# Layer 0 of a convolution sequence: softmax denominators from a column of ones, block transposes on VectorE, and queries among the hidden units

## The chip, the cores and the metric

The kernel runs on one core of a Trainium2 chip. The metric is the device time of one execution in microseconds (us), the median of several runs. One further execution is recorded by the hardware profiler; durations of single instructions come from it.

The engines are TensorE (PE; its weight loads are shown as PEld), VectorE (DVE), ScalarE (ACT), GpSimd (POOL) and SyncE (SP, which here only starts transfers). They run side by side, each in the order of its own program, and wait for each other by semaphores.

## The reference

The input is `x` of 4 x 16 x 512 x 512 float32 (batch, channels, rows, columns). Four layers follow each other; the change touches layer 0 alone, a window attention block with a perceptron:

```python
x = x + depthwise3x3(x) + pos_b                       # position
y = affine(x)                                         # per token, 16 channels
win = 8 x 8 windows of y                              # 64 tokens each
q, k, v = heads(win @ qkv_w.T + qkv_b)                # 2 heads of 8 channels
attn = softmax((q * 8**-0.5) @ k.T)                   # 64 x 64 per window and head
x = x + (attn @ v) @ proj_w.T + proj_b
x = x + gelu(affine(x) @ fc1_w.T + fc1_b) @ fc2_w.T + fc2_b    # 64 hidden units
```

Layer 1 is a quantized 3x3 convolution with batch norm, layer 2 two 3x3 convolutions, layer 3 a convolution with a perceptron. They stand after layer 0 in `conv_layers`.

## The kernel before

`window_attention` computes layer 0 in 64 steps (`STEPS`). A step n takes, of all 4 images, 8 strips of rows and 16 channels, 8 rows by 64 columns: that is 8 windows per strip and image. In the tiles `u` counts the images and `vv` the pairs of strips, four each; `quad(i)` is a group of 32 partitions, two strips (`w`) of 16 channels. `NJ` is 8 windows, `T` 64 tokens, `N` 512.

[...] In the code before, `bank(0)` to `bank(3)` are the halves of two tiles of two banks, `pairs[0]` and `pairs[1]`; `bank(4)` to `bank(7)` are four tiles of one bank, `singles`.

The order of PE, DVE, ACT and SP is the order in which the code is written (`tc.manual_schedule`); the framework adds the semaphore waits. Step n works as follows.

- `values(k)` (k is 0 to 7: `vv = k // 2`, half of the windows) transposes four windows of `y2` on PE (L342) into bank 4 or 6; DVE copies the result to `yt` (L347).
- `scores(k)` multiplies keys by queries (L355), 16 matmuls into banks 0 to 3. ACT takes the exponential of each pair, 1024 elements (L363), to `e`.
- `attend(k)` multiplies `yt` by `e` (L374) into bank 4 or 6, and a matrix of ones, `own`, by `e` (L379) into bank 5 or 7: the denominators, repeated for every channel.
- `divide(k)` takes on ACT a logarithm (L388) and an exponential of its negative (L389), which is the reciprocal, and multiplies on DVE (L390) into `o`.
- `output(*last)` is the second half of the perceptron of step n-1: matmuls by `fc2` (L422), the sum on DVE (L427) into `xo`, and for odd n-1 the stores (`store`, `_store_block`, L92). Each stored block takes two transfers, one for even rows and one for odd.
- `turn_keys` (L314) brings the tokens of the next step into `y2` by transfers within the core.
- `queries(y, h)` computes, for head h, the next step's queries (L324) into banks 0 to 3; DVE empties banks 0 and 2 (L334), ACT banks 1 and 3 (L332), into `g`. It stands once before and once after the last `attend`.
- `project` multiplies `o` by the projection (L398) into banks 4 to 7; DVE adds to `y` (L403).
- Then 16 units of `hidden` (L411), each four matmuls into one of banks 4 to 7 and a gelu on ACT (L416), are strewn among 36 units of `depthwise` (L291), which compute the position term of step n+2 into banks 0 to 3.
- `position` empties banks 0 and 2 on DVE (L306) and 1 and 3 on ACT (L302) into `y`.

Two table loads per step on ACT switch between the exponential and the gelu. On DVE there are two more reductions, of the largest value of `y` (L504, `most`) and of the stored output (L442, `peak`), which later layers need.

## Time and profile before

| | us |
|---|---|
| median of 3 runs | 6021.88 |
| lowest and highest of them | 6014.76, 6022.8 |
| the profiled execution, its own time | 6030.1 |
| the span in its profile | 6028.3 |
| PE busy | 5775.3 (96%) |
| ACT busy | 3837.6 (64%) |
| DVE busy | 3268.4 (54%) |
| POOL busy | 171.1 (3%) |

A line of the timeline gives the start and length in us, the engine, the line of the code, the operation, what it writes and reads with the shapes, and how many instructions of that kind are merged; in brackets, the idle time ahead of it and what ended it. A line of the list of waits gives who waited for whom: us in total, how often, and the longest. A float32 matmul appears as two instructions (two passes). The clock granted to TensorE was 0.993 of full speed on the mean.

### The profile page before, as it was taken

Reading aid. Unit: us, or ns where it says so; the run is one execution under the profiler, and the core shown is the slowest. Engines: PE = TensorE matmul, PEld = TensorE weight load, DVE = VectorE, ACT = ScalarE, POOL = GpSimd, SP = SyncE. Lnnn points to the kernel's source line nnn. Section 1 sums busy time; section 2 is a strip of 40 time slices with the busy share of each in tenths; the row PEclk is TensorE's granted clock in tenths of the full one; section 3 lists DMA queues with packets and bytes.
Section 4 is the critical chain, followed back from the end, with each engine's and each line's share of the span. In section 5 each row is a group of like instructions: output and inputs, shape, how many; then the busy total and the mean of one; then the engine's idle time right before and its main releaser. Section 6 shows DMA issues by size and latency. Waiting matters only on the chain. (4 is left out here: it accounts for less than half of the span.)

```text
span 6028.3 us, 242228 instructions
## 1 busy us (share of the span) xinstructions
PE 5775.3 (96%) x108624; PEld 3084.9 (51%) x108624; DVE 3268.4 (54%) x4648; ACT 3837.6 (64%) x5257; POOL 171.1 (3%) x193
## 2 busy tenths in 40 slices
PE   8999999999999999999999866899999999999999
PEld 5666666666666666666666433333333333333333
DVE  3444444444444444444444455566666666666666
ACT  4777877877787777778777654344444444444444
POOL 0000000000000000000000154000000000000000
PEclk9999999999999999999999999999999999999999
DMA  3233333323333232333333398666676666666663
GB/s 84 58 71 66 64 77 62 78 59 71 67 64 77 61 79 59 71 66 65 77 61 61 58 243 216 163 171 168 167 173 165 168 172 166 168 171 168 167 170 104
DMA packets 638119, 674.57 MB, mean 112 GB/s; under 512 B 371728, under 2 KB 500880, under 8 KB 632976
## 3 DMA queue, kind: packets, MB, share of 16 engines
q1 hardware_dynamic: 635760, 657.53, 47.1%
q8 instruction: 857, 14.04, 1.0%
q0 software_dynamic: 1024, 1.05, 0.1%
q14 instruction: 190, 1.56, 0.1%
q10 hardware_dynamic: 288, 0.39, 0.0%
HBM read 221.15 MB, written 134.48 MB: 59 GB/s over the span
## 5 line engine op out<-in xcount | busy, mean ns | idle before, releaser
L363 ACT ACTIVATE e<-pair 128x1024 f32<-128x1024 f32 x1024 | 992.5, 1021 | 381.7 <-PE pair L355 381.7
L1175 ACT ACTIVATE hid<-tb,vec 128x512 f32<-128x512 f32 x1024 | 620.7, 688 | 517.5 <-PE tb L1167 517.4
L291 PE MATMUL pair<-x,taps 32*32 32x512 f32 x18432 | 927.4, 605 | 2.6 <-ACT y L302 1.2
L1177 DVE TENSOR_SCALAR hid<-tb,vec 128x512 f32<-128x512 f32 x1024 | 695.7, 742 | 2.7 <-PE tb L1167 2.6
L411 PE MATMUL bank<-y,fc_e 32*32 32x512 f32 x8192 | 680.1, 598 | 0.9 <-DVE y L403 0.9
L355 PE MATMUL pair<-g,y 32*128 32x128 f32 x16384 | 653.0, 285 | 26.9 <-ACT y L302 25.0
L355 PEld LDWEIGHTS pair<-g,y 32*128 32x128 f32 x16384 | 542.8, 186 | 215.9 <-issue 108.9
L416 ACT ACTIVATE hid<-bank,f1b 128x512 f32<-128x512 f32 x1024 | 644.5, 686 | 12.4 <-PE bank L411 4.8
L291 PEld LDWEIGHTS pair<-x,taps 32*32 32x32 f32 x18432 | 602.2, 103 | 98.2 <-issue 19.0
L347 DVE COPY yt<-bank 128x512 f32<-128x512 f32 x512 | 347.3, 688 | 540.2 <-PE bank L342 531.9
L1167 PE MATMUL tb<-ye,mat 32*128 32x512 f32 x4096 | 637.6, 624 | 0.3 <-DVE hid L1177 0.3
L374 PE MATMUL bank<-e,yt 128*32 128x128 f32 x16384 | 556.7, 276 | 3.4 <-issue 2.4
L390 DVE TENSOR_TENSOR o<-bank,r 128x512 f32<-128x512 f32 x512 | 354.2, 692 | 372.6 <-ACT r L389 356.3
L379 PE MATMUL bank<-e,hot 128*32 128x512 f32 x4096 | 535.6, 593 | 0.0
L1187 PE MATMUL tb<-hid,mat 128*32 128x512 f32 x4096 | 466.0, 595 | 41.6 <-DVE hid L1177 41.6
L374 PEld LDWEIGHTS bank<-e,yt 128*32 128x32 f32 x16384 | 418.0, 109 | 111.7 <-DVE yt L347 52.8
L306 DVE TENSOR_SCALAR y<-pair,vec 128x512 f32<-128x512 f32 x128 | 90.3, 746 | 706.5 <-PE pair L291 706.5
L1167 PEld LDWEIGHTS tb<-ye,mat 32*128 32x128 f32 x4096 | 267.0, 183 | 323.3 <-issue 219.9
L342 PEld LDWEIGHTS bank<-mat,y 128*128 128x128 f32 x2048 | 216.3, 141 | 376.1 <-issue 270.0
L1092 PE MATMUL tb<-zo,cw 64*32 64x512 f32 x3096 | 362.8, 594 | 14.9 <-issue 8.9
L1092 PE MATMUL tb<-xo,cw 64*32 64x512 f32 x3096 | 366.1, 600 | 10.1 <-issue 7.0
L1092 PE MATMUL tb<-xe,cw 64*32 64x512 f32 x3072 | 361.5, 600 | 0.0
(176 smaller groups left out, 7564.1 us busy)
## 6 DMA issues: line engine op xcount, KB each, us to landing
x<-in_xw_dram SPq DMA_DIRECT2D x32, 2600.0 KB, 10.9
zo<-ze SPq DMA_DIRECT2D x512, 128.5 KB, 2.4
ho<-he SPq DMA_DIRECT2D x512, 128.5 KB, 2.4
xo<-xe SPq DMA_DIRECT2D x512, 128.5 KB, 2.4
y<-y SPq DMA_DIRECT2D x2048, 32.0 KB, 2.2
tx<-x SPq DMA_DIRECT2D x256, 256.0 KB, 4.6
out_dram<-xe SPq DMA_DIRECT2D x128, 512.0 KB, 3.5
x<-xo SPq DMA_DIRECT2D x2016, 32.0 KB, 1.7
```

Source lines behind the costliest of these rows:

```text
L291: nc.tensor.matmul(bank(u)[quad(vv)], taps[quad(u), tap, :], xts[n // 2][quad(u), vv, dy : dy + WS, at : at + BW], start=tap == 0, stop=ta ...
L355: nc.tensor.matmul(bank(u)[:, P * jj : P * jj + P], y2[quad(u), vv, jl + jj].rearrange("p w t -> p (w t)"), g[quad(u), vv, jl + jj].rearra ...
L363: nc.scalar.activation(e[:, 2 * i : 2 * i + 2].rearrange("p u j t -> p u (j t)"), pairs[i], AF.Exp,)
L374: nc.tensor.matmul(b[quad(u), P * jj : P * jj + P], yt[:, jj, quad(u)], e[:, u, jj, :], start=True, stop=True,)
L379: nc.tensor.matmul(d[quad(u)], own, e[:, u].rearrange("p j t -> p (j t)"), start=True, stop=True,)
L411: nc.tensor.matmul(b[quad(k)], fc1[quad(vv), quad(k)], y[quad(vv), u, :], start=True, stop=True,)
L416: nc.scalar.activation(hd, b, AF.Gelu, bias=f1b)
L1092: nc.tensor.matmul(p[r][_quad(2 * f + w)], weights[_half(r), odd, dx, :], src[_half(r), f, dx : dx + W], start=dx == 0, stop=dx == 2,)
L1167: nc.tensor.matmul(p[q], w1[_quad(q), 1 - par, :], inner(src)[_quad(q), f, :], start=True, stop=True,)
L1175: nc.scalar.activation(hd, p[q], AF.Relu, bias=v("l3_b1"))
L1177: nc.vector.tensor_scalar(hd, p[q], v("l3_b1"), 0.0, ALU.add, ALU.max)
L1187: nc.tensor.matmul(p[r][_quad(c)], w2[:, par], hd, start=(r, c) not in seen, stop=(r, c) in seen,)
```

## The change

1. **Denominators.** `yts` are three fixed buffers of three column blocks for each quad: values of strip 0, ones, values of strip 1. A matmul by a neighbouring pair of these blocks gives sums and denominators together. `attend` now takes half the tokens (64 partitions, one strip) per matmul, 32 matmuls instead of 16 and no `own`; the strips go to the two banks of a pair.
2. **Division.** DVE transposes the whole pair in blocks of 32 x 32 (1024 elements per partition), so that tokens lie in the partitions, takes the reciprocal of the 32 denominators, GpSimd multiplies (DVE for k = 7), and `turn_back` transposes 512 elements back into `o`, one turn later. ACT's logarithm and exponential go. Four of eight copies of `values` move to ACT.
3. **PSUM.** Banks 4 to 7 become `pairs[2]` and `pairs[3]`.
4. **Queries.** `query` computes one head and one `vv`, with one DVE instruction to empty it. Eight of them stand among the hidden units; units take the banks 4, 5, 6, 7 in turn.
5. **Depthwise.** 16 of the 36 units move ahead of and behind the last `attend`.
6. **Reductions.** `most` moves behind `project`, `peak` to k = 2, 4, 6 and behind `most`.
7. **Transfers.** Inputs are loaded per step (half the width), stored blocks take one transfer each, spread by `send` over the turns.

```diff
-    n = WS // 2
-    m = r0 // 2
-    for r, mm in ((1, m), (0, m + 1)):
-        (next(queues) if queues else nc.sync).dma_start(
...
+    rows = x1.rearrange("m (r c) b x -> (m r) c b x", r=2)[r0 + 1 : r0 + 1 + WS, :, b, cols]
+    (next(queues) if queues else nc.sync).dma_start(rows.rearrange("m c x -> c m x"), src)
...
-    pairs = [ps.tile([P, 2, 512], F32, name=f"pair{i}") for i in range(2)]
-    singles = [ps.tile([P, 512], F32, name=f"bank{i}") for i in range(4)]
+    pairs = [ps.tile([P, 2, 512], F32, name=f"pair{i}") for i in range(4)]
     def bank(i):
-        return pairs[i // 2][:, i % 2, :] if i < 4 else singles[i - 4]
+        return pairs[i // 2][:, i % 2, :]
...
+    yts = [pa.tile([P, 4 * U, 3, C], F32, name=f"yt{i}") for i in range(3)]
+    for t in yts:
+        nc.gpsimd.memset(t, 1.0)
...
+    def query(y, h, vv, b):
         for u in range(U):
+            nc.tensor.matmul(
+                b[quad(u)], wg[h][quad(vv)], y[quad(vv), u, :], start=True, stop=True
+            )
+        nc.vector.tensor_scalar(
+            g[:, vv, :, h, :], b.rearrange("p (j t) -> p j t", t=T),
+            gb[:, h : h + 1], None, ALU.add,
+        )
...
+        src = b.rearrange("p (a w c) -> p a w c", w=2, c=C)
+        if k in (2, 4, 5, 6):
+            nc.scalar.copy(t[:, :, 0:3:2], src)
+        else:
+            nc.vector.tensor_copy(t[:, :, 0:3:2], src)
...
+    def attend(e, k):
+        t = yts[k % 3]
         for jj in range(4):
             for u in range(U):
+                for w in range(2):
+                    half = slice(64 * w, 64 * w + 64)
+                    nc.tensor.matmul(
+                        bank(4 + 2 * (k % 2) + w)[quad(u), P * jj : P * jj + P],
+                        t[half, U * jj + u, w : w + 2].rearrange("p d c -> p (d c)"),
+                        e[half, u, jj, :],
+                        start=True, stop=True,
+                    )
...
+    def divide(k, n, engine):
+        a = px.tile([P, 1024 + 2 * C], F32, tag="a", name=f"a{n}_{k}")
+        nc.vector.transpose(a[:, 0:1024], pairs[2 + k % 2].rearrange("p w n -> p (w n)"))
...
+        nc.vector.reciprocal(r, low)
+        t = px.tile([P, 16, 2, C], F32, tag="t", name=f"t{n}_{k}")
+        engine.tensor_tensor(
+            t.rearrange("p b w c -> p w b c"), top,
+            r.unsqueeze(3).to_broadcast([P, 2, 16, C]), ALU.mult,
+        )
+        return t
+
+    def turn_back(t, k):
+        nc.vector.transpose(part(o, k), t.rearrange("p b w c -> p (b w c)"))
...
         for k in range(1, 8):
             es[k] = scores(k, n)
             if k > 1:
+                values(k)
+            attend(es[k - 1], k - 1)
+            ts[k - 1] = divide(k - 1, n, nc.gpsimd)
+            if k > 1:
+                turn_back(ts[k - 2], k - 2)
+            if k % 2 and more:
                 turn_keys(ys[n + 1], k // 2)
+            if k in (2, 4, 6):
+                highest_output()
+            send(5)
+        turn_back(ts[6], 6)
+        rounds(1)
+        attend(es[7], 7)
+        turn_back(divide(7, n, nc.vector), 7)
+        rounds(3)
         y = ys.pop(n)
         project(y)
+        if more:
+            highest(n + 1)
+        highest_output()
...
+        hids, asked, units = [], 0, itertools.cycle(range(4, 8))
+        for what in "dddd" + 4 * "hdhqdhdhqd":
+            if what == "h":
                 q = len(hids)
+                hids.append(hidden(y, q, bank(next(units)), n))
...
+            elif what == "q" and more:
+                query(ys[n + 1], asked // V, asked % V, bank(next(units)))
+                asked += 1
+            elif what == "d" and ahead:
+                u = taken.index(min(taken))
+                depthwise(n + 2, taken[u], u)
+                taken[u] += 1
```

More of the change, by code (lines that the diff above doesn't have):

```diff
@@ L87, in _store_block @@
 def _store_block(nc, x1, src, b, r0, cols, queues=None):
-    n = WS // 2
-    m = r0 // 2
-    for r, mm in ((1, m), (0, m + 1)):
-        (next(queues) if queues else nc.sync).dma_start(
-            x1[mm : mm + n, C * r : C * r + C, b, cols].rearrange("m c x -> c m x"),
-            src.rearrange("c (m r) x -> c m r x", r=2)[:, :, 1 - r],
-        )
+    rows = x1.rearrange("m (r c) b x -> (m r) c b x", r=2)[r0 + 1 : r0 + 1 + WS, :, b, cols]
+    (next(queues) if queues else nc.sync).dma_start(rows.rearrange("m c x -> c m x"), src)
 def _store_rows(nc, dst, src, r0):
@@ L188, in load @@
     def load(k):
-        t = xin.tile([P, V, WS + 2, XW + 2], F32, tag="x", name=f"x{k}")
+        t = xin.tile([P, V, WS + 2, BW + 2], F32, tag="x", name=f"x{k}")
         nc.sync.dma_start(t, xw[k])
@@ L193, in window_attention @@
     xts, ys = {0: load(0), 1: load(1)}, {}
-    hot = wts.tile([P, 64], F32, name="hot")
-    nc.sync.dma_start(hot, hots)
-    small, own = hot[:, 0:32], hot[:, 32:64]
+    small = wts.tile([P, 32], F32, name="small")
+    nc.sync.dma_start(small, hots)
     def prod(lhsT, rhs, name, n=P):
@@ L288, in depthwise @@
         dy, dx = divmod(tap, 3)
-        at = BW * (n % 2) + dx
         for vv in range(V):
@@ L292, in depthwise @@
                 bank(u)[quad(vv)], taps[quad(u), tap, :],
-                xts[n // 2][quad(u), vv, dy : dy + WS, at : at + BW],
+                xts[n][quad(u), vv, dy : dy + WS, dx : dx + BW],
                 start=tap == 0, stop=tap == 8,
@@ L319, in turn_keys, with highest, values @@
                 )
-    def queries(y, h):
+    def query(y, h, vv, b):
         for u in range(U):
-            for vv in range(V):
-                nc.tensor.matmul(
-                    bank(vv)[quad(u)], wg[h][quad(vv)], y[quad(vv), u, :],
-                    start=True, stop=True,
-                )
-        for vv in range(V):
-            out = g[:, vv, :, h, :]
-            src = bank(vv).rearrange("p (j t) -> p j t", t=T)
-            if vv % 2:
-                nc.scalar.activation(out, src, AF.Identity, bias=gb[:, h : h + 1])
-            else:
-                nc.vector.tensor_scalar(out, src, gb[:, h : h + 1], None, ALU.add)
-    def values(k, n):
+            nc.tensor.matmul(
[5 more added lines that the diff above has]
+        )
+    def highest(n):
+        nc.vector.tensor_reduce(
+            most[:, n : n + 1], ys[n], AX.XY, ALU.max, apply_absolute_value=True
+        )
+    def values(k):
         vv, jl = k // 2, 4 * (k % 2)
-        b = bank(4 + 2 * (k % 2))
+        b, t = bank(4 + 2 * (k % 2)), yts[k % 3]
         for jj in range(4):
@@ L345, in values @@
             )
-        t = px.tile([P, 4, P], F32, tag="yt", name=f"yt{n}_{k}", bufs=3)
-        nc.vector.tensor_copy(t.rearrange("p j c -> p (j c)"), b)
-        return t
+        src = b.rearrange("p (a w c) -> p a w c", w=2, c=C)
[3 more added lines that the diff above has]
+            nc.vector.tensor_copy(t[:, :, 0:3:2], src)
     def scores(k, n):
@@ L367, in scores @@
         return e
-    def attend(e, yt, k):
-        b, d = bank(4 + 2 * (k % 2)), bank(5 + 2 * (k % 2))
+    def attend(e, k):
+        t = yts[k % 3]
         for jj in range(4):
             for u in range(U):
-                nc.tensor.matmul(
-                    b[quad(u), P * jj : P * jj + P], yt[:, jj, quad(u)], e[:, u, jj, :],
-                    start=True, stop=True,
-                )
-        for u in range(U):
-            nc.tensor.matmul(
-                d[quad(u)], own, e[:, u].rearrange("p j t -> p (j t)"),
-                start=True, stop=True,
-            )
@@ L384, in divide @@
-    def divide(k, n):
-        vv, jl = k // 2, 4 * (k % 2)
-        b, d = bank(4 + 2 * (k % 2)), bank(5 + 2 * (k % 2))
-        r = px.tile([P, 512], F32, tag="r", name=f"r{n}_{k}")
-        nc.scalar.activation(r, d, AF.Ln)
-        nc.scalar.activation(r, r, AF.Exp, scale=-1.0)
-        nc.vector.tensor_tensor(
-            o[:, vv, jl : jl + 4].rearrange("p j h t -> p (j h t)"), b, r, ALU.mult
-        )
+                for w in range(2):
[6 more added lines that the diff above has]
+                    )
@@ new lines, in part @@
+    def part(t, k):
+        vv, jl = k // 2, 4 * (k % 2)
+        return t[:, vv, jl : jl + 4].rearrange("p j h t -> p (j h t)")
+    def divide(k, n, engine):
+        a = px.tile([P, 1024 + 2 * C], F32, tag="a", name=f"a{n}_{k}")
+        nc.vector.transpose(a[:, 0:1024], pairs[2 + k % 2].rearrange("p w n -> p (w n)"))
+        top = a.rearrange("p (w n) -> p w n", w=2)[:, :, 0:512]
+        top = top.rearrange("p w (b c) -> p w b c", c=32)[:, :, :, 0:C]
+        low = a[:, C : 1024 - C].rearrange("p (w n) -> p w n", w=2)[:, :, 0 : 512 - C : 32]
+        r = px.tile([P, 2, 16], F32, tag="r", name=f"r{n}_{k}")
+        nc.vector.reciprocal(r, low)
[3 more added lines that the diff above has]
+            r.unsqueeze(3).to_broadcast([P, 2, 16, C]), ALU.mult,
+        )
+        return t
@@ L405, in project, with hidden @@
             )
-    def hidden(y, q, vv, n):
-        u, b = q // 4, bank(4 + q % 4)
+    def hidden(y, q, b, n):
+        u, vv = divmod(q, 4)
         for k in range(4):
@@ L430, in output, with highest_output, store, send @@
             )
-            if n % 2:
-                store(xo, n // 2, u)
+        if n % 2:
+            store(xo, n // 2, us)
     queues = itertools.cycle((nc.sync, nc.gpsimd))
-    largest = []
-    def store(xo, k, u):
-        i, cb = divmod(k, NQ)
-        largest.append(
-            lambda: nc.vector.tensor_reduce(
-                peak[:, U * k + u : U * k + u + 1], xo[:, u], AX.XY, ALU.max,
-                apply_absolute_value=True,
-            )
-        )
-        for vv in range(V):
-            for w in range(2):
-                r = SR * (2 * vv + w) + WS * i
-                _store_block(
-                    nc, x1, xo[32 * vv + C * w : 32 * vv + C * w + C, u], u, r,
-                    slice(XW * cb, XW * cb + XW), queues if k == STEPS // 2 - 1 else None,
-                )
+    stores, largest = [], []
+    def highest_output(k=1):
+        for _ in range(min(k, len(largest))):
+            xo, i = largest.pop(0)
+            nc.vector.tensor_reduce(
+                peak[:, i : i + 1], xo, AX.XY, ALU.max, apply_absolute_value=True
+            )
+    def store(xo, k, us):
+        i, cb = divmod(k, NQ)
+        for u in us:
+            largest.append((xo[:, u], U * k + u))
+            for strip in range(2 * V):
+                stores.append((xo[C * strip : C * strip + C, u], u, SR * strip + WS * i, cb))
+    def send(k, queues=None):
+        for _ in range(min(k, len(stores))):
+            src, u, r, cb = stores.pop(0)
+            _store_block(nc, x1, src, u, r, slice(XW * cb, XW * cb + XW), queues)
     def bounded():
@@ L475, in window_attention @@
                 mybir.EngineType.PE, mybir.EngineType.DVE, mybir.EngineType.Activation,
-                mybir.EngineType.SP,
+                mybir.EngineType.SP, mybir.EngineType.Pool,
             }
@@ L483, in window_attention @@
                 depthwise(n, tap, u)
+        xts[n + 2] = load(n + 2)
         ys[n] = position(n)
+    highest(0)
     for vv in range(V):
@@ L487, in window_attention @@
     for h in range(NH):
-        queries(ys[0], h)
+        for vv in range(V):
+            query(ys[0], h, vv, bank(vv))
     last, xo = None, None
@@ L491, in window_attention, with rounds @@
     for n in range(STEPS):
-        yts = {k: values(k, n) for k in range(2)}
-        es = {0: scores(0, n)}
+        more, ahead = n + 1 < STEPS, n + 2 < STEPS
+        taken = [0] * U
+        def rounds(k):
+            for i in range(4 * k if ahead else 0):
+                depthwise(n + 2, taken[i % 4], i % 4)
+                taken[i % 4] += 1
+        for k in range(2):
+            values(k)
+        es, ts = {0: scores(0, n)}, {}
         if last:
@@ L498, in window_attention @@
             es[k] = scores(k, n)
-            attend(es[k - 1], yts[k - 1], k - 1)
             if k > 1:
-                yts[k] = values(k, n)
-            divide(k - 1, n)
-            if k == 3:
-                nc.vector.tensor_reduce(
-                    most[:, n : n + 1], ys[n], AX.XY, ALU.max, apply_absolute_value=True
-                )
-            elif largest:
-                largest.pop(0)()
-            if k % 2 and n + 1 < STEPS:
-                turn_keys(ys[n + 1], k // 2)
-        if n + 1 < STEPS:
-            queries(ys[n + 1], 0)
@@ L513, in window_attention @@
-        attend(es[7], yts[7], 7)
-        divide(7, n)
-        if n + 1 < STEPS:
-            queries(ys[n + 1], 1)
+                values(k)
+            attend(es[k - 1], k - 1)
[3 more added lines that the diff above has]
+            if k % 2 and more:
+                turn_keys(ys[n + 1], k // 2)
+            if k in (2, 4, 6):
[3 more added lines that the diff above has]
+        rounds(1)
@@ L517, in window_attention @@
+        attend(es[7], 7)
+        turn_back(divide(7, n, nc.vector), 7)
+        rounds(3)
         y = ys.pop(n)
         project(y)
-        ahead = n + 2 < STEPS
-        if ahead and n % 2 == 0 and n // 2 + 2 < STEPS // 2:
-            xts[n // 2 + 2] = load(n // 2 + 2)
+        if more:
+            highest(n + 1)
+        highest_output()
         if n % 2 == 0:
             xo = px.tile([P, U, WS, XW], F32, tag="xo", name=f"xo{n}", bufs=1)
-        if n + 1 == STEPS:
+        if not more:
@@ L526, in window_attention @@
             flag = bounded()
-        at = [4 + 10 * u + d for u in range(U) for d in (0, 2, 5, 7)]
-        hids, taken = [], [0] * U
-        for i in range(13 * 4):
-            if i in at:
+        hids, asked, units = [], 0, itertools.cycle(range(4, 8))
+        for what in "dddd" + 4 * "hdhqdhdhqd":
+            if what == "h":
                 q = len(hids)
-                hids.append(hidden(y, q, i % 4, n))
-                if n + 1 == STEPS and q in (5, 9, 13):
+                hids.append(hidden(y, q, bank(next(units)), n))
+                if not more and q in (5, 9, 13):
@@ L537, in window_attention @@
                     u = q // 4 - 1
                     output(y, xo, hids[q - 5 : q - 1], (u,), (u,), n)
-            elif ahead:
-                depthwise(n + 2, taken[i % 4], i % 4)
-                taken[i % 4] += 1
-        if n + 1 < STEPS:
+                    send(8, queues)
+            elif what == "q" and more:
[5 more added lines that the diff above has]
+                taken[u] += 1
@@ L543, in window_attention @@
+        if more:
             nc.scalar.preload_act_table_set("natural_log_exp_and_others")
+        if n + 4 < STEPS:
+            xts[n + 4] = load(n + 4)
         if ahead:
@@ L547, in window_attention @@
     output(y, xo, hids[12:], (3,), (3,), n)
-    for f in largest:
-        f()
+    send(8, queues)
+    highest_output(U)
     return nc.values_load(flag[0:1, 0:1], min_val=0, max_val=1)
@@ L1293, in _pack @@
     cws = np.tile(np.concatenate([cws, cws[:, :, ::-1]]), (2, 1, 1, 1, 1))
-    own = np.zeros((2, 64, 2, C))
-    for w in range(2):
-        own[w, :, w, :] = 1.0
-    hots = np.concatenate(
-        [np.tile(np.eye(32), (4, 1)), own.reshape(P, 32)], axis=1
-    ).astype(np.float32)
+    hots = np.tile(np.eye(32), (4, 1)).astype(np.float32)
     padded = np.zeros((B, C, H + 2, W + 2), np.float32)
     padded[:, :, 1 : H + 1, 1 : W + 1] = a["x"]
-    xw = np.zeros((WS, 4, B, 2, C, 4, WS + 2, P + 2), np.float32)
+    xw = np.zeros((WS, 8, B, 2, C, 4, WS + 2, P // 2 + 2), np.float32)
     for i in range(WS):
-        for cb in range(4):
+        for cb in range(8):
             for strip in range(8):
@@ L1311, in _pack @@
                 xw[i, cb, :, w, :, vv] = padded[
-                    :, :, r : r + WS + 2, P * cb : P * cb + P + 2
+                    :, :, r : r + WS + 2, P // 2 * cb : P // 2 * cb + P // 2 + 2
                 ]
@@ L1315, in _pack @@
         "x": a["x"].reshape(B * C, H, W),
-        "xw": xw.reshape(4 * WS, P, 4, WS + 2, P + 2),
+        "xw": xw.reshape(8 * WS, P, 4, WS + 2, P // 2 + 2),
         "mats": mats,
```

## The prediction, made before the changed kernel was built or run

> **What bounds the kernel now.** I read the page first: busy shares, then slices.

> ```profile
> PE 5775.3 (96%) x108624; PEld 3084.9 (51%) x108624; DVE 3268.4 (54%) x4648; ACT 3837.6 (64%) x5257; POOL 171.1 (3%) x193
> PEclk9999999999999999999999999999999999999999
> ```

> TensorE is never idle for long and its clock is full. Layer 0 is the first 3440 us (the last gelu ends at 3439.3); its 64 steps follow each other every 52.67 us (transposes at 1226.23, next at 1278.90). One step in the timeline, PE and ACT: one turn k of attention, then the perceptron.

> ```profile
> 1243.28 1.17 PE L355 MATMUL pair<-g,y 32*128 32x128 f32 x32
> 1244.39 1.08 PE L374 MATMUL bank<-e,yt 128*32 128x128 f32 x32
> 1245.29 1.04 PE L379 MATMUL bank<-e,hot 128*32 128x512 f32 x8
> 1246.26 0.66 PE L342 MATMUL bank<-mat,y 128*128 128x128 f32 x4
> 1244.49 1.94 ACT L363 ACTIVATE e<-pair 128x1024 f32<-128x1024 f32 x2 [0.40 <-PE pair L355]
> 1264.97 2.73 DVE L403 SCALAR_TENSOR_TENSOR y<-bank,pb,y 128x512 f32<-128x512 f32 x4 [0.68 <-PE bank L398]
> 1267.09 10.21 ACT L416 ACTIVATE hid<-bank,f1b 128x512 f32<-128x512 f32 x16
> 1279.50 1.34 ACT L302 ACTIVATE y<-pair,vec 128x512 f32<-128x512 f32 x2 [0.90 <-DVE y L306]
> ```

> A turn takes 3.56 us (1243.28 to 1246.84), all of it matmuls: scores 1.11, attend 0.90, denominators 0.97, transposes 0.58. ACT has 0.40 us to spare. In the perceptron sixteen gelus run without a gap, one per 0.638 us, while PE fills the rest with depthwise taps. From the first sum of `project` (1264.97, call it S) to ACT's half of `position` (1279.50) is **14.53 us**; there the next step's scores are released. PE and ACT are about equally full in it.

> The lines that decide are about PSUM tiles of two banks. In `queries` banks 0 and 1 are halves of one tile `pair0`; DVE empties the even half, ACT the odd.

> ```profile
> 1258.98 1.40 DVE L334 TENSOR_SCALAR g<-pair,gb 128x512 f32<-128x512 f32 x2
> 1259.75 1.35 ACT L332 ACTIVATE g<-pair,gb 128x512 f32<-128x512 f32 x2 [1.42 <-DVE g L334]
> 1260.49 1.37 PE L324 MATMUL pair<-y,wg 32*32 32x512 f32 x18
> ...
> ACT g L332 <- DVE g L334: 182.9, 128, 2.2
> PEld pair L324 <- ACT g L332: 89.6, 128, 2.7
> ```

> ACT could read bank 1 at 1258.98; it waits until DVE has read bank 0 (1259.72). The next matmul into bank 0 could follow at 1259.72; it waits until ACT has read bank 1 (1260.44). It happens 128 times of 128. So the program orders accesses **by the tile, not by the bank**: a write into one half waits for the reader of the other. Banks 4 to 7, where the hidden units lie, are four tiles of their own, and the gelus have no such wait.

> [...] no transpose is in this trace, the nearest row is the 1024-element reduce, 1.21 us. [...]

> **The change: a turn of attention.** PE loses the denominators (0.97). Attend becomes 32 half-height matmuls (64 instructions) instead of 16; with eight tiles at once they take the old 0.9 us (with four, 1.8). A turn's PE work is then 1.11 + 0.58 + 0.95 = 2.65 us. The floor moves to scores-exp-scores: scores and exp share the same two pairs, the exp lasts 1.94 us and PE and semaphores need 1.1 to refill (exp at 1234.12, next at 1237.20): **3.08 us**. ACT loses logarithm and exponential (1.23) and gains four copies per step (0.6 each): fits. DVE per turn: transpose of 1024, 1.2 (the reduce's row[...]); reciprocal of 32 per lane, 0.3 (between 0.23, the 32-element row of `taps`, and 0.45); transpose back, 0.65 (rows of 512). That is 2.15, plus 0.65 in the turns with a copy and 1.15 where `highest_output` comes: 2.9 on average in a step with reductions. Pool's product, 1.2 (at most 2), lies beside it.

> Walked from the first `scores(1)`: before, `o` is ready 30.08 us later (1232.89 to 1262.97). After, exp(7) starts at 1.23 + 6x3.08 = 19.7; attend(6) is seen at 21.4; transpose and reciprocal to 22.95; Pool to 24.3; turn back to 25.0; then divide(7) on DVE alone, 1.25 + 0.3 + 0.7 + 0.7: 27.9. PE's waiting is filled by 16 of the 36 taps. That is 2.2 us earlier. In every other step three reductions delay DVE by about 1.5 us at the end: 29.4, so 0.7 earlier. Mean gain **1.4 us** a step (limits: 3.5, if the tail overlaps better; minus 5, if the transposes take double).

> **The change: the perceptron.** Eight queries join sixteen hidden units in banks 4,5,6,7 in turn, h h q h h q, but these banks are now halves of two pairs. By the rule above a unit waits until the unit before it in its pair has been read, and PE's order turns this into rounds of two units. A unit costs 1.13 us from its first matmul to its reader (two passes of four matmuls):

> ```profile
> 1229.32 3.64 PE L422 MATMUL bank<-hid,mat 128*32 128x512 f32 x32
> 1230.45 0.69 DVE L427 TENSOR_TENSOR xo<-bank,y 128x512 f32<-128x512 f32 x1 [1.81 <-PE bank L422]
> ```

> then a gelu (0.69) or a DVE sum (0.74), then 0.03 to the next matmul. The first unit alone: 1.85. Four rounds of h and q: 1.90 each, 7.6. Four rounds of h and h, whose gelus queue: 1.13 + 0.64 + 0.69 + 0.03 = 2.49 each, 10.0. Three rounds of q and h: 1.90 each, 5.7. Sum 25.1. It starts at S + 1.43 (both sums of pair 2 read). `highest(n + 1)` (2.2) and in every other step `highest_output` (1.15) stand ahead of the first query's sum on DVE: +0.5 or +1.65, mean 1.1. Taps in the same array tiles: +0.3 (0 to 5). The last query starts at S + 27.9, is read at 29.8; DVE's `position` of bank 0 is queued behind it (0.7), ACT's waits for that by the same rule: **S + 30.6** against 14.53, so 16.1 us more (limits 11.5, with rounds of 1.7; 21). The other part of it, gelus and taps, is hidden under the rounds, and the two separate `queries` (about 3 us) that leave attention are inside the 30.08 above.

> At nothing I put the loads of half the width, the single store per block and the memsets ahead of the loop. SP's queue carries them: 64 stores took it 36.00 us before, 0.56 each, and `turn_keys` 0.6 each. With `send` a step of every two issues 32 stores and 32 key transfers, some 40 us, inside a step of 52 or more, and a key transfer stands behind at most a few stores; its reader is the next step's transpose, 25 us or more later. The cover is that distance; gone, a late key would hold PE by 0.6 us per issue ahead of it. Pool's queue gets no transfer in the loop, but DVE's `turn_back` now waits for Pool's product: behind it stand the next turn's transpose and, through the pair it frees, PE's `values`; within the loop the product is a turn old, so only `turn_back(6)` waits (counted above).

> **Sum.** 63 steps x (16.1 - 1.4) = +926; the last step has no queries but sixteen gelus in rounds, +8. The profiled execution took 6030.1 (span 6028.3): 6964. The median of the runs is 8 us below it, so **6956**.

> **Rivals.** *The banks stay independent* (the other side): if the halves of a pair are not ordered, the perceptron keeps its 14.53, as ACT's chain of table load, 16 gelus and table load is the same, and 63 x 1.4 is gained: 5934, **faster**. It decides once the perceptron grows by less than 1.4 us. For it: the gelus run without a gap over the same four banks now. Against it: the 128 waits. *Transposes at half rate*: DVE needs 2.3 + 0.3 + 1.2, with copies and reductions about 4.1 us a turn, attention ends 5 us later than before instead of 1.4 earlier: 63 x 6.4 more, 7360. [...] *Attend gains nothing* (four tiles at once): a turn stays near 3.6, the 1.4 us are lost, 7040. The form exists in the convolutions, so I doubt it. If the array's clock fell in the thinner perceptron, each pass would be longer, above 7400; slices with PE at six tenths still show 9 in PEclk.

> **Chances.** Rounds with transposes at full rate 0.74 (own range 6700 to 7250), with half rate or four tiles 0.14, independent banks 0.10, other 0.02. Independent banks can also end within or above no change, if the reductions ahead of the first query hold the units (1.5 us a step eats the gain), so faster 0.08, same 0.02, slower 0.90, where 0.2% (12 us) is what a measurement of this kernel can tell from no change. The range leaves out the independent banks and the lower clock: 6650 to 7400.

> **What would show it.** Right: gelus in single or double rows with gaps of about 1.2 us that end on PE; PE's units (`hidden`, `query`) waiting for gelus and for DVE's sums over and over; the step near 67 us, PE busy well below nine tenths in layer 0, DVE's transposes near 1.2 and 0.7 us; exp every 3.1 us. Wrong: sixteen gelus in 10 to 12 us (independent banks), transposes of 2.3 us, or a turn of 3.6.

## The result and the profile after

The changed kernel takes **8161.91 us** (median of four runs, 8153.78 to 8166.99) against 6022.34 for the kernel before, a ratio of **1.3548, 95% interval [1.3522, 1.3575]**. The prediction said 6956 and 6650 to 7400. The direction and the place were right, the size was not.

First the page of the changed kernel: busy shares, and the granted TensorE clock in 40 slices.

```profile
span 8165.1 us, 266840 instructions
PE 7463.3 (91%) x120912; PEld 3067.6 (38%) x120912; DVE 4094.9 (50%) x5736; ACT 3243.4 (40%) x4233; POOL 639.6 (8%) x628
PEclk8677677677777777776777777768999999999999
```

The last line is the finding. Before it held only 9s. Now it stands at 6 to 8 over all of layer 0 (whose last gelu ends here at 5586 us) and returns to 9 behind it. A slice lasts 204 us and a step 86, so it mixes stages. The windows view takes them apart: one attention stage and one perceptron stage of a step (columns: PE, PEld, DVE, ACT, POOL busy with the number of instructions, then granted clock, DMA share, GB/s), first of the kernel before, then of the changed one.

```profile
1233.00:1264.00 31.00, 31.00 (x671) 19.26 (x672) 19.35 (x24) 24.67 (x33) 0.00 (x0) 1.00 0.33 62
1265.00:1279.00 14.00, 14.00 (x429) 11.11 (x410) 2.98 (x5) 12.68 (x19) 0.00 (x0) 1.00 0.29 44
```
```profile
2239.00:2269.00 30.00, 28.65 (x942) 20.21 (x939) 20.56 (x29) 15.48 (x18) 7.42 (x7) 1.00 0.20 39
2272.00:2316.00 44.00, 39.39 (x314) 8.62 (x311) 9.27 (x11) 12.98 (x19) 0.00 (x0) 0.53 0.01 1
```

In attention the clock stays at 1.00. In the perceptron it is 0.53, and that stage has grown from 14 to 44 us. PE's busy time doesn't show it: 39.39 of 44 us look like nine tenths. The count does: 314 matmul records in 44 us, against 429 in 14.

The timeline of the changed kernel, first in attention, answers to the turn shown before.

```profile
2242.12 0.35 DVE L391 RECIPROCAL r<-a 128x32 f32<-128x32 f32 x1
2242.59 1.94 ACT L359 ACTIVATE e<-pair 128x1024 f32<-128x1024 f32 x2 [1.21 <-PE pair L351]
2242.62 1.06 POOL L393 TENSOR_TENSOR t<-a,r 128x512 f32<-128x512 f32 x1 [64.95 <-DVE r L391]
2244.39 1.25 DVE L386 STREAM_TRANSPOSE a<-pair 128x1024 f32<-128x1024 f32 x1 [1.92 <-PE pair L372]
2245.66 1.94 ACT L359 ACTIVATE e<-pair 128x1024 f32<-128x1024 f32 x2 [0.65 <-PE pair L351]
```

A turn takes 3.07 us here (2242.59 to 2245.66). The block transpose of 1024 elements, the reciprocal and Pool's product have, to within 0.15 us, the durations that the sum used. Then the perceptron of the same step:

```profile
2269.03 2.72 DVE L411 SCALAR_TENSOR_TENSOR y<-pair,pb,y 128x512 f32<-128x512 f32 x4 [2.26 <-PE pair L406]
...
2273.01 0.61 PE L419 MATMUL pair<-y,fc_e 32*32 32x512 f32 x4
...
2278.86 1.08 PE L419 MATMUL pair<-y,fc_e 32*32 32x512 f32 x4
...
2284.58 1.99 PE L419 MATMUL pair<-y,fc_e 32*32 32x512 f32 x16
...
2286.29 1.93 PE L286 MATMUL pair<-x,taps 32*32 32x512 f32 x8
2286.58 0.69 ACT L424 ACTIVATE hid<-pair,f1b 128x512 f32<-128x512 f32 x1 [2.21 <-PE pair L419]
2288.36 0.69 ACT L424 ACTIVATE hid<-pair,f1b 128x512 f32<-128x512 f32 x1 [1.09 <-remote]
...
2314.82 0.69 ACT L297 ACTIVATE y<-pair,vec 128x512 f32<-128x512 f32 x1 [2.26 <-DVE y L301]
```

S is 2269.03 and ACT's `position` 2314.82: 45.8 us, where 14.5 was before and 30.6 was predicted. Gelus stand singly, with gaps that end on PE. The same four matmuls of 512 columns last 0.61 us at 2273.01 and 1.08 at 2278.86: between them the clock has halved (its own record has it from 2275.08, 6 us after S). At 2284.58 two hidden units enter together; the first has its gelu at 2286.58, the second only at 2288.36, when the depthwise unit between the two in the program (2286.29) has ended. And the waits view shows the ordering by the pair (engine, waiting line, released by: us in total, times, longest).

```profile
ACT hid L424 <- PE pair L419: 904.1, 394, 3.4
...
PEld pair L318 <- ACT hid L424: 658.8, 252, 3.1
...
PEld pair L419 <- ACT hid L424: 371.7, 260, 3.1
```

The first row is the gelus that wait for a hidden unit. The other two are units that wait for a gelu to read the other half of their pair: 252 is 4 in each of 63 steps.

### The profile page after: what moved, and what is told of

Its sections match the earlier page's. It is cut to its first block, busy times and chain, and to the rows that moved or that the text cites. A ratio compares the mean times of both kernels' runs of the same rounds, so it can differ in the third digit from the quotient of the medians.

```text
span 8165.1 us, 266840 instructions
## 1 busy us (share of the span) xinstructions
PE 7463.3 (91%) x120912; PEld 3067.6 (38%) x120912; DVE 4094.9 (50%) x5736; ACT 3243.4 (40%) x4233; POOL 639.6 (8%) x628
## 5 line engine op out<-in xcount | busy, mean ns | idle before, releaser
L286 PE MATMUL pair<-x,taps 32*32 32x512 f32 x18432 | 2146.9, 778 | 3.7 <-issue 1.8
L419 PE MATMUL pair<-y,fc_e 32*32 32x512 f32 x8192 | 1395.4, 1002 | 137.5 <-ACT hid L424 64.2
L321 DVE TENSOR_SCALAR g<-pair,gb 128x512 f32<-128x512 f32 x512 | 383.5, 750 | 2188.0 <-PE pair L419 1247.8
L424 ACT ACTIVATE hid<-pair,f1b 128x512 f32<-128x512 f32 x1024 | 702.6, 687 | 1876.0 <-PE pair L419 904.1
L318 PE MATMUL pair<-y,wg 32*32 32x512 f32 x4096 | 936.7, 1009 | 229.1 <-ACT hid L424 221.8
L393 POOL TENSOR_TENSOR t<-a,r 128x512 f32<-128x512 f32 x448 | 474.3, 1059 | 5046.8 <-DVE r L391 5046.8
L386 DVE STREAM_TRANSPOSE a<-pair 128x1024 f32<-128x1024 f32 x512 | 635.2, 1241 | 351.2 <-PE pair L372 296.1
L372 PE MATMUL pair<-e,yt 64*32 64x128 f32 x32768 | 600.5, 274 | 26.6 <-DVE xo L435 19.8
L372 PEld LDWEIGHTS pair<-e,yt 64*32 64x32 f32 x32768 | 457.8, 106 | 159.4 <-issue 98.0
L336 PE MATMUL pair<-mat,y 128*128 128x128 f32 x2048 | 378.3, 322 | 45.5 <-DVE a L386 39.0
L1118 PE MATMUL tb<-zo,cw 64*32 64x512 f32 x3096 | 363.0, 595 | 14.8 <-issue 8.9
```

The lines of the kernel that those rows point to most:

```text
L286: nc.tensor.matmul(bank(u)[quad(vv)], taps[quad(u), tap, :], xts[n][quad(u), vv, dy : dy + WS, dx : dx + BW], start=tap == 0, stop=tap == 8,)
L318: nc.tensor.matmul(b[quad(u)], wg[h][quad(vv)], y[quad(vv), u, :], start=True, stop=True)
L372: nc.tensor.matmul(bank(4 + 2 * (k % 2) + w)[quad(u), P * jj : P * jj + P], t[half, U * jj + u, w : w + 2].rearrange("p d c -> p (d c)"), ...
L386: nc.vector.transpose(a[:, 0:1024], pairs[2 + k % 2].rearrange("p w n -> p (w n)"))
L419: nc.tensor.matmul(b[quad(k)], fc1[quad(vv), quad(k)], y[quad(vv), u, :], start=True, stop=True,)
L424: nc.scalar.activation(hd, b, AF.Gelu, bias=f1b)
```

## The experiments

All step parts below are means over the steps of one traced execution, in us: from the first `exp(1)` to S (the first sum of `project`), from S to ACT's `position`, and from there to the next `exp(1)`. Ratios are to the kernel before, run on the same chip. The time is the median of the runs; the traced executions of e1, e2 and e12 took 51, 40 and 31 us less than their medians.

| kernel | exp(1) to S | S to position | position to exp(1) | clock over the span | time | ratio and interval |
|---|---|---|---|---|---|---|
| before | 30.98 | 14.56 | 7.29 | 0.993 | 6022.34 | |
| changed | 30.30 | 46.80 | 9.30 | 0.812 | 8161.91 | 1.3548 [1.3522, 1.3575] |
| e1_own_banks | 29.75 | 21.80 | 7.56 | 0.965 | 6475.3 | 1.0754 [1.0723, 1.0785] |
| e2_before_with_pairs | 31.22 | 28.04 | 7.29 | 0.939 | 6954.11 | 1.1540 [1.1459, 1.1622] |
| e3_filler | 30.31 | 33.23 | 8.65 | 0.968 | 7283.76 | 1.2087 [1.2057, 1.2118] |
| e4_taps_moved | 30.31 | 42.99 | 9.17 | 0.823 | 7936.38 | 1.3170 [1.3137, 1.3204] |
| e5_sums_first | 29.71 | 18.48 | 7.51 | 0.986 | 6238.84 | 1.0353 [1.0322, 1.0383] |
| e6_rows_apart | 29.77 | 16.69 | 8.29 | 0.979 | 6159.95 | 1.0213 [1.0182, 1.0245] |
| e7_denominators | 32.17 | 16.56 | 7.55 | 0.965 | 6248.29 | 1.0363 [1.0333, 1.0394] |
| e8_rotation | 29.74 | 16.50 | 8.25 | 0.980 | 6139.38 | 1.0186 [1.0160, 1.0212] |
| e9_denominators_rows | 31.74 | 14.53 | 7.35 | 0.973 | 6090.83 | 1.0113 [1.0076, 1.0150] |
| e10_queries_on_act | 29.03 | 14.50 | 7.36 | 0.990 | 5901.44 | **0.9807 [0.9785, 0.9829]** |
| e11_filler12 | 30.32 | 47.29 | 9.24 | 0.816 | 8179.67 | 1.3557 [1.3488, 1.3625] |
| e12_filler24 | 30.31 | 39.79 | 9.22 | 0.895 | 7751.68 | 1.2847 [1.2724, 1.2970] |

### The pairs: e1 and e2

e1 is the changed kernel with banks 4 to 7 as tiles of their own, e2 the kernel before with them as pairs and nothing else changed.

```
e1  -    pairs = [ps.tile([P, 2, 512], F32, name=f"pair{i}") for i in range(4)]
    +    pairs = [... for i in range(2)]
    +    singles = [ps.tile([P, 512], F32, name=f"bank{i}") for i in range(4)]
    -        nc.vector.transpose(a[:, 0:1024], pairs[2 + k % 2].rearrange("p w n -> p (w n)"))
    +        for w in range(2):
    +            nc.vector.transpose(a[:, 512 * w : 512 * w + 512], bank(4 + 2 * (k % 2) + w))
e2  the same edit of pairs and singles the other way round
```

> The changed kernel with banks 4 to 7 as four tiles of their own again; divide transposes the two banks one after the other (two transposes of 512 instead of one of 1024, about 0.1 us more per turn). Theory (halves of a pair are ordered, units then go in rounds, the array falls idle and its clock halves): both effects go together; the perceptron, 45.8 us from the first sum of project to ACT's position in the changed kernel, takes 15 to 18 us, the clock stays above 0.97, total 6060 us (5980 to 6150). Rival (the queries' work on DVE, or the array's clock falling for a reason in attention, sets the stage): above 7400 us.

> The kernel before with one edit: banks 4 to 7 become the halves of two pairs, nothing else. Theory: the sixteen hidden units go in rounds of two, about 2.5 us each at full clock and 4 at half: the stage grows from 14.5 us to 25 (total 6700) or, with the clock halved, to 36 (total 7400). Rival (the pairs alone do no harm, it takes the queries among the units): 6022 us.

e1 takes away nearly four fifths of the loss (1687 of 2140 us) by the tiles alone (and the division's transpose in two halves that goes with them), and e2 puts some 930 us on the kernel before by the tiles alone. So the pairs are the first cause: the same units, in the same order, then wait where a bank's neighbour in the tile is unread. In e2 S to position is 24.8 us in just over half of the steps, as expected, and 27.3 to 33.3 in the others, most often 32.7 (36 was expected at half clock): the clock again. e1 stayed 325 us above the range expected of it: 19.2 us in every odd step, but 20.3 to 28 in the even ones. Its windows, an even and an odd step:

```profile
1880.00:1904.00 24.00, 22.78 (x316) 9.68 (x304) 9.86 (x12) 11.62 (x18) 0.00 (x0) 0.72 0.26 49
1936.00:1955.00 19.00, 18.91 (x435) 9.00 (x408) 12.08 (x16) 8.85 (x12) 0.00 (x0) 1.00 0.07 13
```

and the timeline of the even one:

```profile
1881.06 2.28 DVE L328 TENSOR_REDUCE most<-y 128x1 f32<-128x2048 f32 x1
...
1883.25 1.21 DVE L452 TENSOR_REDUCE peak<-xo 128x1 f32<-128x1024 f32 x1
1884.38 1.40 DVE L322 TENSOR_SCALAR g<-bank,gb 128x512 f32<-128x512 f32 x2
...
1885.17 1.08 PE L421 MATMUL bank<-y,fc_e 32*32 32x512 f32 x8 [1.22 <-DVE g L322]
1887.04 0.69 ACT L426 ACTIVATE hid<-bank,f1b 128x512 f32<-128x512 f32 x1 [3.10 <-PE bank L421]
```

Two reductions stand on VectorE ahead of the first query's sum. PE waits for that sum's bank, and ACT waits 3.10 us for the fifth gelu. Behind the hole the clock is halved, as the first window shows. The row at 1885.17 merges eight passes, and each of them takes 0.92 to 1.00 us, where 0.61 is the length at full clock. In odd steps the second reduction isn't there.

### The clock: e3, e11 and e12

These add matmuls with zero weights to the changed kernel, accumulated into banks that taps are being summed in, so that the numbers don't change.

```
+    none = wts.tile([P, 32], F32, name="none")        # zeros
+    def filler(n, u):
+        for vv in range(V):
+            nc.tensor.matmul(bank(u)[quad(vv)], none[quad(u)],
+                xts[n][quad(u), vv, 0:WS, 0:BW], start=False, stop=False)
-        for what in "dddd" + 4 * "hdhqdhdhqd":
+        for what in "dddd" + 4 * "hdfffhqdfffhdhfffqd":   # e3; e11 has f, e12 ff
```

> The changed kernel with up to 36 more units of matmuls per step among the hidden units and queries, by a matrix of zeros into the depthwise sums, so that results stay as they are: extra work on the array, nothing taken away. Theory (half of the lost time is the clock[...]): the clock stays near 1 and the stage shrinks from 45.8 to 32 to 36 us, total 7400 us (7200 to 7650). Rival (the latencies between the units set the time, whatever the clock reading): 8160 to 8700 us.

> e3_filler with 12 of its 36 zero-weight units per step, one at each of the twelve places (the results don't change). Theory (the clock is granted or halved as a whole, by how much the array does over a few microseconds): one unit at each place is too little, S to ACTpos stays at 44 to 49 us and the clock near half in it, the time is 8,000 to 8,300 us. Rival (each unit of work counts alike): a third of e3's gain, S to ACTpos near 42.3, the time near 7,870.

> The same with 24 units, two at each place. Theory (all or nothing): either as e3 (S to ACTpos 31.5 to 33.5 us at full clock, 7,170 to 7,290 us) or as the changed kernel (8,000 to 8,300), or steps of both kinds and few between. Rival (alike): two thirds of the gain, S to ACTpos near 37.8 in nearly every step, the time near 7,580.

e3 adds work to the busiest engine and the kernel is 878 us faster. S to position takes 32.9 to 33.9 us in all its steps. With a third of these units (e11) nothing is gained; with two thirds (e12) there are steps of two kinds, near 33 and near 48.4 us, and of 62 only one lies well between (36.7). Windows of e3, then of two successive steps of e12:

```profile
2279.00:2312.00 33.00, 31.54 (x609) 13.55 (x597) 12.14 (x15) 13.56 (x18) 0.00 (x0) 1.00 0.24 37
```
```profile
2313.00:2361.00 48.00, 44.57 (x513) 13.80 (x492) 12.30 (x15) 13.56 (x18) 0.00 (x0) 0.59 0.16 24
2400.00:2432.50 32.50, 29.72 (x529) 10.53 (x510) 11.29 (x14) 13.56 (x18) 0.00 (x0) 0.98 0.01 3
```

In these runs the clock is full or half, and matmuls whose results nothing needs raised it: 0.968 over the span in e3, 0.812 in the changed kernel. The record of the clock in all fourteen traces has the values 1.00 and 0.50 alone, and between the first and the last change each value is held for a whole multiple of 3.41 us. A stage can fall late: seven of e11's steps take some 41 us, and in them the clock falls 17 us after S.

How much work can be read off from stage means: matmul records from S to position, over the time that such a step takes at full clock. The changed kernel has 340 in what would be some 33 us, 10 per us: it falls 3.5 to 6.3 us after S in every step but the last, where it is half ahead of S already. e11 has 436, some 13: it falls in every step too. e12 has 15.5, e2 16.6, e1's even steps 17.4: both kinds occur. e3 has 18.1 and falls in the last 2.6 us at most; e1's odd steps 18.4, e5 19.1, the kernel before 28.5: none falls between S and position. In these stages the edge lies near **17 passes of 32x512 per us**, an estimate from these figures. At full clock the two passes of e10's first hidden unit start 0.46 us apart (2039.99 and 2040.45), so that is seven or eight passes at work at once on average, an estimate too. Near the edge a hole decided: e12's steps at half clock are, but for the start, even ones, which have the second reduction ahead of the first query's sum.

Windows cut at the clock's own stretches of 3.41 us tell load from pauses. Four of them from the changed kernel around S (2269.03), then four in one line from e2 at half clock:

```profile
2264.86:2268.27 3.41, 2.83 (x85) 1.07 (x87) 1.81 (x4) 0.00 (x0) 0.00 (x0) 1.00 0.16 30
2268.27:2271.69 3.42, 3.15 (x70) 0.97 (x41) 2.66 (x5) 1.17 (x1) 0.00 (x0) 1.00 0.02 5
2271.69:2275.10 3.41, 3.08 (x40) 0.65 (x40) 2.92 (x3) 1.49 (x3) 0.00 (x0) 1.00 0.00 0
2275.10:2278.51 3.41, 2.84 (x24) 0.43 (x8) 0.00 (x0) 1.14 (x2) 0.00 (x0) 0.50 0.00 0
```
```profile
1501.80:1515.50 13.70, 13.70 (x192) 5.07 (x165) 0.00 (x0) 5.06 (x8) 0.00 (x0) 0.50 0.00 1
```

Behind the first stretch, with PE idle for 0.58 us but 85 records in it, the clock holds. Behind the third, with PE idle for only 0.33 us but 40 records, it is halved. In e2 it stays halved though PE has no idle moment. Counted over layer 0 of all fourteen traces (from 130 us on), in the stretches at full clock that hold nothing but 32x32 matmuls: with 60 or more of them started, none of 3468 was followed by half clock; with 32 to 59, 315 of 1001; with fewer, 89 of 90. Sixty in 3.41 us are 17.6 per us, the same edge. So what sorts these stretches is the number of matmuls; PE's idle time in those shown does not.

### The taps between two hidden units: e4

```
-        for what in "dddd" + 4 * "hdhqdhdhqd":
+        for what in "dddd" + 4 * "hdhqddhhqd":
```

> The changed kernel with the order of units hdhqddhhqd instead of hdhqdhdhqd: no depthwise unit stands between two hidden units of one round. Theory (a matmul's completion is reported in program order, so a hidden unit behind a depthwise unit of the same rows of the array as the unit ahead is seen two passes late): a round of two hidden units shrinks by 1.1 us (half clock), four per step: total 7880 us (7750 to 8000). Rival (the gelus' queue sets the round): 8160 us, same.

S to position is 3.8 us shorter, and the time lies in the range given. The second gelu of an h-h round now starts 0.59 us after the first (29.13 and 29.72 us from S in a step of e4), where it was 1.78 in the changed kernel (41.27 and 43.05). The clock is nearly as low (0.823 over the span, 0.812 in the changed kernel), so this is the depthwise unit's own share: it stood between two hidden units, and the second of them was signalled only behind its end. In the trace of the changed kernel this shows 248 times: the second gelu follows the first by 1.77 us and PE's signal by 0.02 us at the median.

### The order of VectorE's sums, and the array's rows: e5, e6, e8

e5 is e1 with `highest(n + 1)` behind the second query and `highest_output()` behind the fifth:

```
-        if more:
-            highest(n + 1)
-        highest_output()
...
                 asked += 1
+                if asked == 2:
+                    highest(n + 1)
+                elif asked == 5:
+                    highest_output()
```

> The changed kernel with the eight PSUM banks apart again (as in e1_own_banks) and with its two reductions behind project taken from in front of the first query's sum: most's behind the second query's sum, peak's behind the fifth. Theory: what e1 kept of the loss is the fifth gelu's stall (the first query's sum 3.5 us late behind the two reductions, its bank late by as much) and, in the even steps, where both reductions run, the clock that falls in that hole. Then S to ACTpos is 18 to 19.2 us in even and odd steps alike, the granted clock above 0.985, and the time 6,120 to 6,220 us. Rival: the clock falls for another reason (units still ending too late for ACT); the even steps stay at 25 us or more and the time at 6,350 to 6,450.

S to position is 18.5 us in even and odd steps, and 236 us are gained: the reductions' place was what e1 had kept of the fallen clock. The time is 19 us above the upper end that was expected.

e6 gives each depthwise unit rows that no neighbour has; e8 gives all units the rows i mod 4 (`hidden(y, q, i % 4, ...)`, `query(..., i % 4, ...)`, `u = i % 4`).

> As e5_sums_first, and each depthwise unit in the rounds takes the rows of the array that no hidden or query unit right beside it in the program uses, instead of the least advanced of the four. Theory: a unit in the rows of its neighbours stands behind them and, since PE's completions come in program order, keeps a gelu waiting; then S to ACTpos is 16.3 to 17.6 us, 64 to 140 us off e5's time. Rival: with banks of their own the units are late for no row, ACT and the banks set the pace; then S to ACTpos is within 0.4 us of e5's and the time within 25 us.

> As e5_sums_first, and all units of the rounds take the array's rows in turn: unit number i of the program, whether hidden, query or depthwise, takes rows i mod 4 (the order of the kernel before, where hidden did so; the changed kernel gives hidden q rows q mod 4, whatever stands beside it). No unit then has a neighbour within three in its rows. Theory (rows): S to ACTpos is 15.3 to 16.4 us in even and odd steps, ACTpos to the next exp(1) 7.3, the time 6,050 to 6,130. Rival: what e6_rows_apart gained was all that rows can give (16.66 us); the time is within 30 us of its 6,160.

Rows gain 1.8 us in e6, as expected, and no more in e8 (16.50): there the rival held, the time is within 21 us of e6's. In both the next step's start is late instead: position to `exp(1)` takes 8.9 to 9.0 us in two thirds of e6's odd steps and in more than half of e8's, and 7.3 in nearly all the rest, as before. A window of e8's units, then two stretches of the clock in the opening of the next step:

```profile
1743.00:1759.00 16.00, 15.14 (x369) 7.22 (x352) 11.89 (x15) 12.58 (x18) 0.00 (x0) 1.00 0.40 75
1758.80:1762.21 3.41, 1.77 (x37) 1.43 (x40) 2.58 (x5) 2.06 (x4) 0.00 (x0) 1.00 0.91 268
1762.21:1765.62 3.41, 3.41 (x20) 0.87 (x16) 0.69 (x1) 1.76 (x2) 0.00 (x0) 0.50 0.39 163
```

The units have 21 passes per us, and the clock falls behind them all the same, for a single stretch of 3.41 us: in the stretch before it PE is busy for only 1.77 us, because the next scores wait 1.47 us for ACT's `position`. So the dense stage didn't keep the clock up behind the thin stretch that followed it (37 records in 3.41 us).

### The denominators without the rest: e7, e9, e10

e7 keeps the ones in the values, the lanes' division, the stores and loads of the change, but takes banks of their own, `queries` in two groups around the last attend, and the order of the taps as before.

> The denominators alone: values with ones, the lanes' division, stores and loads as changed, but the eight banks apart, the queries in two groups around the last attend and the depthwise units in the order that they had before. Theory: the attention part of the change is a gain that the other two parts hide: seven turns of 3.08 to 3.15 instead of 3.56 us take 2.9 to 3.4 us off exp1 to S (27.4 to 28 us with the queries in it), S to ACTpos stays at 14.5 to 14.8, the clock above 0.985, and the time is 5,790 to 5,870 us, faster than before. Rival: the end of the attention (the last transpose, reciprocal, product and transpose back, 3 us in a row on VectorE ahead of project) gives it back: exp1 to S 30 us or more and 5,960 to 6,050 us.

The expectation failed on both parts. exp(1) to S is 32.17 us and S to position 16.56. The timeline of e7 at the end of attention:

```profile
2013.16 0.71 DVE L417 STREAM_TRANSPOSE o<-t 128x512 f32<-128x512 f32 x1 [0.66 <-POOL t L410]
2013.80 1.37 DVE L340 TENSOR_SCALAR g<-pair,gb 128x512 f32<-128x512 f32 x2
2014.54 1.34 ACT L338 ACTIVATE g<-pair,gb 128x512 f32<-128x512 f32 x2 [5.03 <-DVE g L340]
2015.09 1.30 DVE L403 STREAM_TRANSPOSE a<-bank 128x512 f32<-128x512 f32 x2
```

VectorE waits for Pool, then sums queries, and only at 2015.09 begins the last turn's transposes, though ACT has been idle since the last exp. So the lane division and queries with sums on VectorE stand in each other's way. The clock falls here as well: 61 times in 60 steps, always between `exp(1)` and S, each time behind a stretch in which PE stands still for 1.6 us or more. How much of the 32.17 us is the clock's wasn't measured. e9 changes one thing in e7, the rows of a hidden unit: `i % 4` as before, in place of `q % 4`.

> e7_denominators with one edit: its hidden units take rows i mod 4 as in the kernel before (e7 had left them at q mod 4). Theory: that alone was why e7's S to ACTpos was 16.55 and not 14.54; it goes to 14.4 to 14.8, exp1 to S stays at 31 to 33, and the time is 6,090 to 6,150 us. Rival: the two reductions behind project or the narrower loads cost it; then S to ACTpos stays above 16.

S to position is 14.53 us: the rows were all of that part (e7 had kept the changed kernel's). e10 then rearranges the end, in two edits at once:

```
-            if vv % 2:
+            if vv % 2 or h == 0:
                 nc.scalar.activation(out, src, AF.Identity, bias=gb[:, h : h + 1])
...
-        turn_back(ts[6], 6)
         if more:
             queries(ys[n + 1], 0)
         attend(es[7], 7)
-        turn_back(divide(7, n, nc.vector), 7)
+        last7 = divide(7, n, nc.vector)
+        turn_back(ts[6], 6)
+        turn_back(last7, 7)
```

> e9_denominators_rows with the end of the attention rearranged: the first query group's four sums all on ScalarE (idle there from the last exp to the gelus' table load), and VectorE's last block transposes, reciprocal and product ahead of the transpose back of turn 6, which waits for Pool. Theory: in e7 the query sums stood on VectorE in the middle of the lane division and held the last turn up (exp1 to S 32.2 us instead of 28 or less); with them out of the way exp1 to S is 27.8 to 29.5 us, S to ACTpos 14.4 to 15, and the time 5,890 to 5,980 us, faster than the kernel before. Rival: PE's second query group, waiting for ScalarE's sums, is late in front of project instead; exp1 to S 30 us or more and 6,010 to 6,100.

```profile
2032.01 2.42 ACT L338 ACTIVATE g<-pair,gb 128x512 f32<-128x512 f32 x4 [1.31 <-PE pair L330]
...
2033.61 1.26 DVE L403 STREAM_TRANSPOSE a<-bank 128x512 f32<-128x512 f32 x2
...
2041.31 10.17 ACT L441 ACTIVATE hid<-bank,f1b 128x512 f32<-128x512 f32 x16
```

In e10's timeline the four sums of the first group lie on ACT while VectorE goes on with the transposes, and the sixteen gelus run in one row of 10.17 us, as they did before. exp(1) to S is 29.03 us, within what was expected, and the clock doesn't fall in these steps. The time, **5901.44 us, beats the kernel before** by 1.9% [1.7%, 2.2%]: the change is a gain once the division in lanes has neither pairs nor queries in its way. e10 also keeps the change's loads, single stores and places of the reductions, and what these are worth by themselves wasn't run; nor were its two edits run apart.

## Why the prediction was wrong in size

Per step the changed kernel takes 33.6 us more (86.43 against 52.83; times 64 steps 2150; 2140 were measured). S to position has 32.2 of it, position to exp(1) 2.0, and exp(1) to S is 0.7 shorter.

- **The rounds by pair: right.** The waits, the single gelus and the built e1 and e2 show them. Their size: at full clock (e3) S to position is 33.2 where 30.6 was predicted, with e3's extra units in it.
- **The clock: the step that failed.** The prediction set it aside with "slices with PE at six tenths still show 9 in PEclk" and left it out of the range. Those two slices (3466 to 3768 us) lie behind layer 0, each is a mean over 151 us, and a 9 stands for 0.90 or more. In finer windows the same trace of before has the clock at half in one of them:

```profile
3743.00:3766.90 23.90, 6.02 (x61) 2.83 (x69) 13.04 (x20) 6.64 (x7) 0.00 (x0) 0.50 0.42 104
```

  So the evidence was misread, and PE's busy share said nothing of a stage in which PE looks busy with few matmuls (39.39 of 44 us, 314 records). The clock costs 46.8 - 33.2 = 13.6 us of the 32.2 in a step, some 860 of the 1206 us by which the prediction fell short. The thin filling could be counted beforehand: sixteen hidden, eight query and twenty depthwise units in its own 30.6 us are 352 passes, 11.5 per us, where the trace of before showed 429 records in 14 us. How thin a stage may become was not in that trace, since its clock holds from 73.7 us to the end of layer 0.
- **"Taps in the same array tiles: +0.3 (0 to 5)": too small, within its bounds.** e4 gains 3.8 us by moving one of them in each group, at the halved clock. The prediction took PE's order for the starts of matmuls as well as for their ends. In the changed kernel's trace the ends agree and the starts don't: the second hidden unit's matmuls start at 2284.65, 1.6 us ahead of the depthwise unit that the program puts before them (2286.29), and PE signals them at 2288.33, behind that unit's end. In e3, at full clock, the second gelu of an h-h round comes 0.92 us behind the first (at 23.28 and 22.35 us from S in one step) where 0.64 to 0.69 were taken; the four hidden units of a group take 6.85 us where the three rounds of the prediction make 6.29. Four groups are 2.2 us of the 2.6 missing; that it is the depthwise unit alone was shown at half clock only.
- **The reductions ahead of the first query, +1.1 on average: right in kind.** Where the clock holds, e1's even and odd steps differ by 1.1 us (20.3 and 19.2). What they cost beyond it, through the clock, wasn't foreseen.
- **Attention: prices right, gain half.** Turn 3.08 predicted, 3.07 measured; transpose 1.2 and 1.25, reciprocal 0.3 and 0.35, Pool 1.2 (the author's estimate) and 1.06; attend, for which 0.9 was taken with eight tiles at once and 1.8 with four, gives way to the next scores after 1.08. (In the convolutions of before, passes of the same height, 64x512, start eight in 0.43 us, 3999.73 to 4000.16, and last 0.61 us each.) The gain of exp(1) to S was to be 1.4 on average, 2.2 without reductions and 0.7 with; it is 0.7 on average, by the medians 1.2 without and none with (30.89 us in even steps, 29.61 in odd ones, 30.85 before). The end of it has `project` waiting among the taps (VectorE waits 2.26 us for the first sum at 2269.03, 0.68 before); this was seen, not tested.
- **Not in the sum at all**: position to exp(1), 2.0 us longer. The step opens at the halved clock: its mean in this part is 0.74 in the changed kernel, 0.81 in e3 (8.65 us), 0.97 in e5 (7.51) and 1.00 before (7.29).
- **The rivals.** Transposes at half rate and attend with four tiles fell with the durations (1.25 us, not 2.3; 1.08 us, not 1.8). The banks that stay independent, built as e1, ended not at 5934 but at 6475: the perceptron doesn't keep its 14.5 us, since rows, reductions, queries and the clock take 7.2.

A rough account of the 32.2 us from S to position, by differences of the table: 13.6 the clock (changed to e3), 14.7 pairs and reductions at full clock, with e3's extra units in it (e3 to e5), 2.0 the rows (e5 to e8), 1.9 what is left with eight queries among the units (e8 to before). The last wasn't tested by itself.

## What to carry to other kernels

Before PSUM banks are joined into one tile for the sake of a wider instruction, list who else writes and reads these banks: ordered by the tile, a queue of four became rounds of two here, and e2 lost some 930 us. Count the matmuls per microsecond of a stage, not PE's busy share, and compare with stages whose clock is known: the perceptron, thinned out from 31 matmul records per us to 7, lost nearly half the clock (0.53 on the mean), and a pass of 512 columns went from 0.61 to 1.08 us. Read the clock in windows of a few us, since a slice of the page (151 us before) hid a fall. Put VectorE's long reductions, for which nothing waits, behind the first sums that release a bank (236 us in e5).
